# Turning two weight matrices by chunks of rows as they load, in a random-feature attention and MoE kernel

## The chip, the cores and the metric

The kernel runs on one core of one Trainium2 chip. The metric is device time in microseconds from one launch to its end; lower is better. The span in a profile runs from the first to the last instruction of one profiled execution. In this text TensorE is also called PE (and PEld for its weight loads), VectorE DVE, ScalarE ACT, GpSimd POOL and SyncE SP, as the profile does.

## The reference

The input `x` has 4 x 2048 tokens of width 512, normalized to `xn`. The output is `x + attention(xn) + ffn(xn)`. The attention part turns tokens and 512 input-weight rows into 512 random features and multiplies them; the ffn part is a mixture of 64 experts with 8 chosen for each token, plus one shared expert.

```python
def _rfs(xw, ab, AB, gs):
    dot_products = jnp.einsum('...d,rd->...r', xw, ab[:, None] * gs)
    correction = (0.5 * jnp.sum(xw * xw, axis=-1))[..., None] * (ab * ab)
    return 1.0 / math.sqrt(NUM_RFS) * AB * jnp.exp(dot_products - correction)

weights = _rfs(input_weights, xis, jnp.exp(xis), proj_matrix)
feats   = _rfs(xn,            xis, jnp.exp(xis), proj_matrix)
attention = jnp.einsum('bsr,or->bso', feats, weights)

# ffn: sigmoid router, 4 of 8 groups, top 8 of 64 experts, capacity 256 each
g = jnp.einsum('ech,ehi->eci', dispatch, gate_w)
u = jnp.einsum('ech,ehi->eci', dispatch, up_w)
expert_out = jnp.einsum('eci,eih->ech', jax.nn.silu(g) * u, down_w)
sg = jax.nn.silu(tokens @ shared_gate_w) * (tokens @ shared_up_w)
output = scattered_and_weighted(expert_out) + sg @ shared_down_w
```

## The kernel before

Every matrix product is made of three products of `float32r` operands: each operand is split into a high part (`upper`, L98, a cast on ScalarE) and the remainder (`rest`, L101, a subtraction on VectorE), and `products` (L108) adds high by high, high by low and low by high.

Tokens are worked in 16 blocks of 512 rows (`TB`), each of 4 chunks of 128 rows (`NS`); the width of 512 is 4 column chunks (`KC`). Work comes in this order.

*Start.* The input weights `wi` load in four DMAs of 128 rows each, the projection `pj` in two of 256 rows, then token blocks 0 and 1 (`xb`), the router weights `rw_sb` and the shared expert's weights `sgu` and `sd`, all issued from SyncE's queue in this order. GpSimd builds the identity `ident`, a triangle `tri`, ones, and small index tables. `statistics(wi)` (L275, L278) takes means and variances of `wi` on VectorE. `turn` (L331) turns a 512 x 512 matrix: for each column chunk `kc` it makes four transposes, one for each chunk of rows, into one tile of 512 columns in PSUM, and then splits that tile into `hi[kc]` and `lo[kc]`. It is called for `wi`, giving `wT`, and for `pj`, giving `pT`. `projected` multiplies the two into four tiles `ps_f`, one for each chunk `rc` of 128 features. Meanwhile VectorE takes block 0's statistics and inverse roots (`roots`), which are placed behind the last `rest` of `pT`; ScalarE makes the normalized rows `xw` from `shift` (L290, L301); and `turn` is called for them. `as_row` and `across` send a row of squared norms through DRAM (`norms`, L262) and read it back across all partitions as `q` (L267); for the weights this tile is `wn`. `exponent` (L493) on `wn`, an exponential, a scale and one more split (`features_w`) make the attention weights `fW`, in four pieces of their own.

*Dense phase.* For even blocks `dense` computes the shared expert (`ps_gu`, `ps_o`), the features (`ps_f`) and the attention output; `look_up` does the routing, whose logits go through `ps_l`, `lt` (L374) and back through `ps_lt` (L381). Odd blocks are only routed and their turned tiles stored in DRAM (`turned`).

*Experts.* 64 experts are worked one after another: loads of gate and up weights two experts ahead and of down weights one ahead, splits, gathering of tokens, `ps_gu`, `ps_e`, and adding rows into the output. The features of the odd blocks (`ps_fu`, `ps_y`) are computed between them. The last block and the stores end the kernel.

*What sets the order.* The program is written step by step, and a scheduler puts each engine's instructions into one fixed order, with a semaphore wait where data or a buffer is needed; an engine works through its own order and never passes a waiting instruction. `behind(a, b)` adds an order without data between two instructions; `last["upper"]` and `last["rest"]` hold the latest splits for that purpose. Most tiles of 4 KiB a partition (`kib4`) come from one pool, `four`, with `SLOTS4` = 40 slots that are given out again when their tile is read for the last time; a load into a slot waits for that. `wT`, `pT` and `fW` take four slots each: `wT`'s come back after `projected`, those of `pT` and `fW` never. The pool `act` has four buffers with the tag `t`, used by `lt` and other short-lived tiles; `q` has three buffers.

The piece of `turn` that the change replaces for the two weight matrices:

```python
for kc in range(KC):
    pr = pool.tile([P, TB], dt, tag=tag, name="ps_x")
    for s in range(NS):
        last["turn"] = nc.tensor.transpose(pr[:, ts(s, P)], src(s)[:, ts(kc, P)], ident)
    last["upper"] = upper(hi[kc], ps)
    last["rest"] = rest(lo[kc], ps, hi[kc])
```

Of the kernel before, what the change touches and what calls it, by code (L numbers as in the profile page):

```python
# [9 lines left out]
FP = mybir.dt.float32  # L10
FPR = mybir.dt.float32r
I32 = mybir.dt.int32
# [6 lines left out]
P = 128  # L19
# [3 lines left out]
E = 64  # L23
# [8 lines left out]
TB = 512  # L32
NB = T // TB
NS = TB // P
KC = H // P
RC = R // P
IC = I // P
NH = CAP // P
SLOTS4 = 40
UT = TB // 2  # L40
GAP = 5
NCH = T // P
ROUND = 5
TE = 4
TPAD = T + CAP
XW = H + E + 1
# [7 lines left out]
def rfs_attention_moe_kernel(  # L54
# [15 lines left out]
    nc = tc.nc  # L70
    xf = x.flatten_outer_dims()

    const = ctx.enter_context(tc.tile_pool(name="const", bufs=1))
    dram = ctx.enter_context(tc.tile_pool(name="dram", bufs=1, space=DRAM))
    ps_tr = ctx.enter_context(tc.tile_pool(name="ps_tr", bufs=2, space=PSUM))
    ps_mm = ctx.enter_context(tc.tile_pool(name="ps_mm", bufs=4, space=PSUM))
    ps_sm = ctx.enter_context(tc.tile_pool(name="ps_sm", bufs=2, space=PSUM))

    four = ctx.enter_context(tc.tile_pool(name="four", bufs=SLOTS4))
    rows = ctx.enter_context(tc.tile_pool(name="rows", bufs=4))  # L80
    rt = ctx.enter_context(tc.tile_pool(name="rt", bufs=1))
    act = ctx.enter_context(tc.tile_pool(name="act", bufs=4))

    def kib4(shape, name, dt=FPR):
        return four.tile(shape, dt, tag="four", name=name)
# [11 lines left out]
    def upper(dst, src):  # L97
        return nc.scalar.copy(dst, src)  # L98

    def rest(dst, src, hi, on=nc.vector):  # L100
        return on.tensor_tensor(dst, src, hi.bitcast(FP), ALU.subtract)  # L101
# [15 lines left out]
    def behind(a, b):  # L117

        tc.add_manual_dep(a.ins, b.ins.name, ORDER, reason="what a needs comes late")
# [23 lines left out]
    def load_rows(src, name, at_once=2):  # L143

        xb = Chunks(NS, name, FP)
        for k, t in enumerate(xb.t):
            for s in range(0, 2, at_once):
                r0 = (2 * k + s) * P
                nc.sync.dma_start(
                    t[:, s : s + at_once, :],  # L150
                    src[r0 : r0 + at_once * P, :].rearrange("(s p) d -> p s d", p=P),
                )
        return xb

    def load_tokens(b):
        return load_rows(xf[ts(b, TB), :], "xb")
# [8 lines left out]
    last = {}  # L165
    late_blocks = range(1, NB - 1, 2)
    last_stored = late_blocks[-1]
    wi = load_rows(iw, "wi", 1)
    pj = load_rows(proj, "pj")
    xbs = {0: load_tokens(0)}  # L170
    ab = const.tile([P, RC], FP, name="ab")
    nc.sync.dma_start(ab, xis.rearrange("(c p) -> p c", p=P))
    rw_sb = kib4([P, KC, E], "rw_sb", FP)
    nc.sync.dma_start(rw_sb, rw.rearrange("(c p) e -> p c e", p=P))

    def load_shared_gates():
# [15 lines left out]
    ident = const.tile([P, P], FP, name="ident")  # L192
    make_identity(nc, ident)
    ident_r = const.tile([P, P], FPR, name="ident_r")
    nc.gpsimd.tensor_copy(ident_r, ident)
    tri = kib4([P, P], "tri", FP)
    make_upper_triangular(nc, tri, 1.0, diag=True)
    tri_r = const.tile([P, P], FPR, name="tri_r")
    nc.gpsimd.tensor_copy(tri_r, tri)
# [15 lines left out]
    nc.gpsimd.iota(slot_i, pattern=[[P, NH]], base=0, channel_multiplier=1)  # L215
    slot = const.tile([P, NH], FP, name="slot")
    nc.gpsimd.tensor_copy(slot, slot_i)
    erow_i = kib4([P, E], "erow_i", I32)
    nc.gpsimd.iota(erow_i, pattern=[[1, E]], base=-E, channel_multiplier=0)
    erow = const.tile([P, E], FP, name="erow")  # L220
    nc.gpsimd.tensor_copy(erow, erow_i)
# [41 lines left out]

    def across(n):

        q = rt.tile([P, TB], FP, tag="q", name="q", bufs=3)
        nc.sync.dma_start(q, norms[n].partition_broadcast(P))  # L267
        return q

    def statistics(rows_of, after=NS * [None]):  # L270

        mv = rt.tile([P, NS, 2], FP, tag="mv", name="mv", bufs=2)
        for s in range(NS):
            st = rt.tile([P, 6], FP, tag="st", name="st", bufs=4)
            last["stats"] = nc.vector.bn_stats(st, rows_of[s])  # L275
            if after[s] is not None:
                behind(last["stats"], after[s])
            nc.vector.bn_aggr(mv[:, s, :], st)  # L278
        return mv
# [17 lines left out]
    def normalize(b, rstd, shift):  # L297
# [11 lines left out]
        xc = None  # L309
        if b >= ROUND:  # L310

# [10 lines left out]
    def turn(src, name, pools=((ps_tr, "tr"),), after=None, dt=FP):  # L322

        hi = Chunks(KC, name + "_h")
        lo = Chunks(KC, name + "_l")
        for kc in range(KC):
            pool, tag = pools[kc % len(pools)]
            pr = pool.tile([P, TB], dt, tag=tag, name="ps_x")
            ps = pr if dt is FP else pr.bitcast(FP)
            for s in range(NS):  # L330
                last["turn"] = nc.tensor.transpose(  # L331
                    pr[:, ts(s, P)], src(s)[:, ts(kc, P)], ident if dt is FP else ident_r
                )
                if after is not None:
                    behind(last["turn"], after)
                    after = None
            last["upper"] = upper(hi[kc], ps)
            last["rest"] = rest(lo[kc], ps, hi[kc])
        return hi, lo

    xTs = {}

    def look_up(b):

        xw, xc = normed.pop(b)
        xT = turn(
            (lambda s: xc[s // NH][:, s % NH, :].bitcast(FPR))
            if xc
# [166 lines left out]
    def dense(b, xT, whole, w, rows_of):  # L515


        (sgu_h, sgu_l), (sd_h, sd_l) = w
        nsq = across(b) if whole else None
        hT = [kib4([P, IC, TB], "hT") for _ in range(2)]  # L520
        v = parts(xT, KC)
# [55 lines left out]
    def late_attention(blocks):  # L577

        blocks = list(blocks)
        nxt = fetch_block(blocks[0]), across(blocks[0])  # L580
        yield
        for n, b in enumerate(blocks):
            xu, nsq = nxt
            fT = Chunks(RC, "fU"), Chunks(RC, "fU")
            for rc in range(RC):
                ps = ps_sm.tile([P, TB], FP, tag="sm", name="ps_fu")
                feature(fT, parts(xu, KC), nsq, rc, ps)
                yield
            if n + 1 < len(blocks):
                nxt = fetch_block(blocks[n + 1]), across(blocks[n + 1])  # L590
            for s in range(NS):
                if s % 2 == 0:
                    yb = kib4([P, 2, H], "yb", FP)
                po = ps_sm.tile([P, H], FP, tag="sm", name="ps_y")
                attended(po, fT, s, True)
                last["dve"] = nc.vector.tensor_copy(yb[:, s % 2, :], po)
                if "down" in last:
                    behind(last["dve"], last["down"])
                if s % 2:
                    r0 = (b // 2) * TB + (s // 2) * UT  # L600
                    nc.sync.dma_start(
                        attn[r0 : r0 + UT, :].rearrange("(s p) d -> p s d", p=P), yb
                    )
                yield
# [10 lines left out]
        added.append(group)  # L615


    wmv = statistics(wi)
    wT = turn(lambda s: wi[s], "wT", ((ps_tr, "tr"), (ps_sm, "sm")))
    wq = const.tile([P, NS], FP, name="wq")  # L620
    nc.gpsimd.tensor_tensor(wq, wmv[:, :, 0], wmv[:, :, 0], ALU.mult)
    nc.gpsimd.tensor_tensor(wq, wq, wmv[:, :, 1], ALU.add)
    nc.gpsimd.tensor_scalar(padded[2][:, :NS], wq, -0.5 * H, None, ALU.mult)
    as_row(NB, padded[2])
    wn = across(NB)
    pT = turn(lambda s: pj[s], "pT", ((ps_mm, "mm"),))
    rwp = const.tile([P, KC, 2, E], FPR, name="rwp")
    behind(upper(rwp[:, :, 0, :], rw_sb), last["upper"])
    rest(rwp[:, :, 1, :], rw_sb, rwp[:, :, 0, :], nc.gpsimd)
# [6 lines left out]
    def split(t, name, after=(None, None)):  # L636

        hi, lo = kib4(list(t.shape), name + "_h"), kib4(list(t.shape), name + "_l")
        both = upper(hi, t), rest(lo, t, hi)
        last["split"] = both[1]  # L640
        for a, b in zip(both, after):
            if b is not None:
                behind(a, b)
        return hi, lo

    def split_gates(gu):
        return list(zip(*(split(t, "gu") for t in gu)))

    def split_down(d):
        return split(d, "d")  # L650

    sgate = split(sgu[0], "gu", (None, seed1))
    ps_w = []
    for rc in range(RC):
        pool, tag = ((ps_sm, "sm"), (ps_tr, "tr"))[rc // 2]
# [16 lines left out]
    lt0 = last["lt"]  # L672
    shared_w = list(zip(sgate, sup)), split(sd, "d", (lt0, exponents))
    next(late)
    fW = Chunks(RC, "fW_h"), Chunks(RC, "fW_l")

    def features_w(rc):
        f = fw[rc]
# [18 lines left out]
    def find(at, e):  # L697

        for h in range(NH):
            in_turn(  # L700
                nc.gpsimd.indirect_dma_start(  # L701
                    out=at[:, e % TE, h, :],
                    out_offset=None,
# [5 lines left out]
    def tokens_of(n, at, after):  # L709


        sl = slot.unsqueeze(1).to_broadcast([P, TE, NH])
        less = nc.vector.tensor_tensor(
            at, at, sl.unsqueeze(3).to_broadcast([P, TE, NH, P]), ALU.is_le
        )
        behind(less, after)
        tok = rt.tile([P, TE, NH], FP, tag="tok", name="tok", bufs=2)
        nc.vector.tensor_reduce(tok, at, AX.X, ALU.add)
        nc.vector.tensor_tensor(tok, tok, first_of[:, ts(n, TE), :], ALU.add)
        own = rt.tile([P, TE, NH], FP, tag="sown", name="sown", bufs=2)  # L720
        nc.vector.scalar_tensor_tensor(own, tok, float(T), sl, ALU.is_ge, ALU.mult)
# [278 lines left out]
```

## Time and profile before

| what | value |
|---|---|
| median of 3 runs | 1310.99 us (1310.63 to 1311.27) |
| the profiled execution's own time | 1310.94 us |
| its span | 1309.2 us |
| TensorE busy | 1296.7 us, 99% of the span |
| VectorE busy | 925.0 us, 71% |
| ScalarE busy | 645.2 us, 49% |
| GpSimd busy | 581.7 us, 44% |
| granted TensorE clock, mean | 0.999 |

The profiled execution took 1310.94 us, of which 1309.2 are its span and 1.7 lie around it. A row of the timeline gives start and duration of an instruction, or of several equal ones in a row (x4), and in brackets how long the engine stood idle before it and what ended that. A matmul's duration includes its way through the array, and equal ones overlap: their pace is the distance between starts. A row of the waits gives the waiting instruction, what released it, the time in total, how often, and the longest.

### The profile page before, as it was taken

How to read it: one execution, taken by the hardware profiler on the slowest of the kernel's cores; microseconds unless marked ns; L12 is line 12 of the kernel's file. 1: busy time of each engine (PE TensorE's matmuls, PEld its weight loads, DVE VectorE, ACT ScalarE, POOL GpSimd, SP SyncE). 2: the span in 40 equal slices, each digit the busy share in tenths (PEclk: the TensorE clock that was granted, in tenths of full speed). 3: DMA queues.
4: the chain of work that ended last, by engine and by line, in shares of the span. 5: the costliest groups of instructions: out<-in, count | busy, mean ns of one | idle time of the engine just before them, and what ended most of it. 6: DMA issues, size and time to landing. Idle time of an engine off the chain costs nothing.

```text
span 1309.2 us, 21368 instructions
## 1 busy us (share of the span) xinstructions
PE 1296.7 (99%) x7648; PEld 1138.6 (87%) x7648; DVE 925.0 (71%) x1922; ACT 645.2 (49%) x1017; POOL 581.7 (44%) x692
## 2 busy tenths in 40 slices
PE   8999999999999999999999999999999999999998
PEld 6888888888888999999999999999999999988886
DVE  7978768867865776777767677776776676643555
ACT  5643544354432555656566556555665566540111
POOL 3122022123106767877666667767676654210000
PEclk9999999999999999999999999999999999999999
DMA  7665675675586989999999999999999999784995
GB/s 255 242 213 205 244 279 199 238 286 212 201 307 193 317 226 330 259 290 272 304 282 266 292 272 274 246 321 262 282 256 303 280 261 233 206 239 168 318 319 193
DMA packets 189498, 338.61 MB, mean 259 GB/s; under 512 B 15952, under 2 KB 87632, under 8 KB 189392
## 3 DMA queue, kind: packets, MB, share of 16 engines
q1 hardware_dynamic: 153456, 245.93, 54.6%
q0 software_dynamic: 35936, 91.32, 29.7%
q8 instruction: 60, 0.98, 0.3%
q14 instruction: 46, 0.38, 0.1%
HBM read 220.66 MB, written 104.99 MB: 249 GB/s over the span
## 4 chain that ended last, share of the span: by engine, by line
PE 91%; DVE 4%; DMA 2%; SPq 1%; ACT 1%; issue 1%; POOL 0%; DVEq 0%; ACTq 0%
PE ps_gu L108 41%; PE ps_e L108 13%; PE ps_o L108 13%; PE ps_y L108 6%; PE ps_fu L108 6%; PE ps_f L108 4%; PE ps_t L771 3%; PE ps_x L331 2%; PE ps_l L364 2%; DMA xb<-in_L_attn_x_dram 1%; DVE st L275 1%; DMA xT_l<-turned 1%; SPq L262 1%; DVE xT_l L101 1%; DMA gu<-in_L_ffn_up_w_dram 0%
## 5 line engine op out<-in xcount | busy, mean ns | idle before, releaser
L824 POOL DMA_INDIRECT out_dram<-ye,who x128 | 225.3, 1760 | 189.3 <-ACT ye L823 140.9
L108 PE MATMUL ps_gu<-gT,gu_h 128*128 128x256 f32 x2048 | 290.0, 283 | 0.0
L108 PEld LDWEIGHTS ps_gu<-gT,gu_h 128*128 128x128 f32 x2048 | 267.2, 191 | 5.6 <-ACT gu_h L98 1.0
L701 POOL DMA_INDIRECT at<-upto,line x128 | 138.0, 1078 | 76.0 <-DVE first_of L695 37.3
L108 PE MATMUL ps_gu<-gT,gu_l 128*128 128x256 f32 x1024 | 167.0, 285 | 0.0
L101 DVE TENSOR_TENSOR gu_l<-gu,gu_h 128x1024 fp32r<-128x1024 f32 x128 | 155.7, 1218 | 6.9 <-ACT gu_h L98 6.9
L754 POOL DMA_INDIRECT xg<-xnw,who x128 | 137.3, 1073 | 39.0 <-issue 32.0
L108 PE MATMUL ps_e<-d_h,ehT 128*128 128x512 f32 x512 | 148.5, 391 | 0.0
L108 PEld LDWEIGHTS ps_gu<-gT,gu_l 128*128 128x128 f32 x1024 | 140.7, 191 | 0.3
L98 ACT CAST gu_h<-gu 128x1024 fp32r<-128x1024 f32 x128 | 132.4, 1058 | 0.0
L98 ACT CAST ehT<-sg 128x512 fp32r<-128x512 f32 x64 | 39.7, 621 | 156.3 <-DVE sg L501 156.3
L823 ACT ACTIVATE ye<-ps_e,we 128x512 f32<-128x512 f32 x128 | 88.6, 694 | 57.0 <-PE ps_e L108 56.1
L108 PEld LDWEIGHTS ps_e<-d_h,ehT 128*128 128x128 f32 x512 | 94.7, 188 | 18.8
L246 POOL TENSOR_TENSOR a<-rstd,ve 128x4 f32<-128x4 f32 x45 | 10.5, 233 | 200.1 <-DVE rstd L242 197.6
L501 DVE SCALAR_TENSOR_TENSOR sg<-sg,ps_gu 128x512 f32<-128x512 f32 x64 | 43.9, 686 | 68.4 <-PE ps_gu L108 68.0
L507 ACT ACTIVATE f<-f,ab 128x512 f32<-128x512 f32 x64 | 46.3, 723 | 82.0 <-DVE f L493 81.3
L101 DVE TENSOR_TENSOR d_l<-d,d_h 128x1024 fp32r<-128x1024 f32 x64 | 78.2, 1222 | 7.8 <-ACT d_h L98 7.4
L101 DVE TENSOR_TENSOR gT<-ps_t,gT 128x512 fp32r<-128x512 f32 x128 | 83.2, 682 | 0.2 <-ACT gT L98 0.2
L101 DVE TENSOR_TENSOR ehT<-sg,ehT 128x512 fp32r<-128x512 f32 x64 | 44.3, 692 | 51.5 <-ACT ehT L98 51.5
L108 PE MATMUL ps_o<-fW_h,fT 128*128 128x512 f32 x288 | 80.0, 392 | 0.2 <-ACT fT L98 0.2
L108 PE MATMUL ps_e<-d_l,ehT 128*128 128x512 f32 x256 | 79.3, 391 | 0.0
L108 PE MATMUL ps_o<-d_h,hT 128*128 128x512 f32 x256 | 79.1, 396 | 0.0
(181 smaller groups left out, 2526.8 us busy)
## 6 DMA issues: line engine op xcount, KB each, us to landing
gu<-in_L_ffn_gate_w_dram SPq DMA_DIRECT2D x64, 512.0 KB
gu<-in_L_ffn_up_w_dram SPq DMA_DIRECT2D x64, 512.0 KB
d<-in_L_ffn_down_w_dram SPq DMA_DIRECT2D x64, 512.0 KB
xnw<-xw SPq DMA_DIRECT2D x32, 577.0 KB
xb<-in_L_attn_x_dram SPq DMA_DIRECT2D x32, 512.0 KB
out_dram<-xb SPq DMA_DIRECT2D x32, 512.0 KB
xT_h<-turned SPq DMA_DIRECT2D x30, 512.0 KB
xT_l<-turned SPq DMA_DIRECT2D x30, 512.0 KB
```

What stands on the lines that cost most here:

```text
L98: return nc.scalar.copy(dst, src)
L101: return on.tensor_tensor(dst, src, hi.bitcast(FP), ALU.subtract)
L108: last["pe"] = nc.tensor.matmul(ps, w[c][a], v[c][b], start=(start and part == 0 and c == 0), stop=(stop and part == 2 and c == n - 1),)
L331: last["turn"] = nc.tensor.transpose(pr[:, ts(s, P)], src(s)[:, ts(kc, P)], ident if dt is FP else ident_r)
L364: logits = nc.tensor.matmul(pl, rwp[:, kc].rearrange("p t e -> p (t e)"), v[kc], start=(n == 0 and kc == 0), stop=(n == 1 and kc == KC - 1),)
L501: nc.vector.scalar_tensor_tensor(dst, dst, 0.5, u, ALU.mult, ALU.mult)
L507: nc.scalar.activation(f, f, AF.Exp, scale=ab[:, rc : rc + 1])
L701: nc.gpsimd.indirect_dma_start(out=at[:, e % TE, h, :], out_offset=None, in_=upto, in_offset=bass.IndirectOffsetOnAxis(ap=line[:, e, h : h ...
L754: nc.gpsimd.indirect_dma_start(out=xgs[e][:, h, :], out_offset=None, in_=xnw, in_offset=bass.IndirectOffsetOnAxis(ap=who[:, e, h : h + 1], ...
L771: turned_s = nc.tensor.transpose(pr[:, c, ts(h, P)], xr[:, h, ts(c2 * 2 + c, P)], ident_r)
L823: nc.scalar.activation(ye[:, h, :], po, AF.Copy, scale=wes[e][:, h : h + 1])
L824: now = nc.gpsimd.indirect_dma_start(out=out, out_offset=bass.IndirectOffsetOnAxis(ap=who[:, e, h : h + 1], axis=0), in_=ye[:, h, :], in_o ...
```

## The change

`wi` and `pj` are now turned chunk of rows by chunk of rows. A new function, `turn_as_loaded`, makes the four transposes of one chunk of 128 rows, one for each column chunk, into one PSUM tile, and splits it into the 128 columns `ts(s, P)` of `hi` and `lo`. Its outputs are tiles of 4 x 512 in the pool of constants, written 128 columns at a time in each of the four column chunks. `pj` loads in four DMAs of 128 rows. Ahead of the first chunk stand ten transposes of the identity into a PSUM tile that nobody reads. `statistics(wi)` is now written behind both turns. `fW` takes the place of `wT` once `wT` has been used. To make room, `four` has 33 slots instead of 40, `rw_sb`, `tri` and `erow_i` are taken from `act`, and `q` has two buffers. `split` now also records its `upper` in `last`, so that what is placed behind the latest `upper` may come behind that one.

```diff
-SLOTS4 = 40
+SLOTS4 = 33
+WARM = 10
...
-    pj = load_rows(proj, "pj")
+    pj = load_rows(proj, "pj", 1)
...
-    rw_sb = kib4([P, KC, E], "rw_sb", FP)
+    rw_sb = act.tile([P, KC, E], FP, tag="t", name="rw_sb")
...
-    tri = kib4([P, P], "tri", FP)
+    tri = act.tile([P, P], FP, tag="t", name="tri")
...
-    erow_i = kib4([P, E], "erow_i", I32)
+    erow_i = act.tile([P, E], I32, tag="t", name="erow_i")
...
-        q = rt.tile([P, TB], FP, tag="q", name="q", bufs=3)
+        q = rt.tile([P, TB], FP, tag="q", name="q", bufs=2)
...
+    def turn_as_loaded(src, hi, lo, pools):
+        for s in range(NS):
+            pool, tag = pools[s % len(pools)]
+            ps = pool.tile([P, KC, P], FP, tag=tag, name="ps_x")
+            for kc in range(KC):
+                last["turn"] = nc.tensor.transpose(ps[:, kc, :], src[s][:, ts(kc, P)], ident)
+            to = hi[:, :, ts(s, P)], lo[:, :, ts(s, P)]
+            last["upper"] = upper(to[0], ps)
+            last["rest"] = rest(to[1], ps, to[0])
...
+    warm = ps_mm.tile([P, TB], FP, tag="mm", name="ps_0")
+    for n in range(WARM):
+        nc.tensor.transpose(warm[:, ts(n % NS, P)], ident, ident)
+    wT = [const.tile([P, KC, TB], FPR, name=f"wT_{n}") for n in "hl"]
+    turn_as_loaded(wi, *wT, ((ps_tr, "tr"), (ps_sm, "sm")))
+    wT = [[t[:, c, :] for c in range(KC)] for t in wT]
+    pT = [const.tile([P, KC, TB], FPR, name=f"pT_{n}") for n in "hl"]
+    turn_as_loaded(pj, *pT, ((ps_mm, "mm"),))
+    pT = [[t[:, c, :] for c in range(KC)] for t in pT]
     wmv = statistics(wi)
-    wT = turn(lambda s: wi[s], "wT", ((ps_tr, "tr"), (ps_sm, "sm")))
...
     wn = across(NB)
-    pT = turn(lambda s: pj[s], "pT", ((ps_mm, "mm"),))
...
-        last["split"] = both[1]
+        last["upper"], last["split"] = both
...
-    fW = Chunks(RC, "fW_h"), Chunks(RC, "fW_l")
+    fW = wT
```

## The prediction

> **What bounds the kernel now.** I read the page's busy shares, then who TensorE waits for over the whole span, then the start engine by engine, since the diff edits mostly the start.
>
> ```profile
> PE 1296.7 (99%) x7648; PEld 1138.6 (87%) x7648; DVE 925.0 (71%) x1922; ACT 645.2 (49%) x1017; POOL 581.7 (44%) x692
> ```
>
> TensorE is busy 1296.7 of 1309.2 us, so only 12.5 us are idle. Its waits, longest in total first (engine, line waited for: us in total, times, longest):
>
> ```profile
> PE ps_x L331 <- DMA wi<-_attn_input_weights_dram: 5.1, 3, 3.7
> PE ps_bu L445 <- DVE prior_r L435: 0.9, 3, 0.3
> PE ps_lt L381 <- ACT lt L374: 0.6, 2, 0.4
> ```
>
> The only large named wait is at the very start. TensorE's own timeline there (start us, us, line, out<-in, count):
>
> ```profile
> 3.67 1.02 PE L331 MATMUL ps_x<-ident,wi 128*128 128x128 f32 x2 [3.67 <-DMA wi<-_attn_input_weights_dram]
> 5.89 0.47 PE L331 MATMUL ps_x<-ident,wi 128*128 128x128 f32 x1 [1.20 <-DMA wi<-_attn_input_weights_dram]
> 6.56 3.04 PE L331 MATMUL ps_x<-ident,wi 128*128 128x128 f32 x13 [0.20 <-DMA wi<-_attn_input_weights_dram]
> 9.39 3.29 PE L331 MATMUL ps_x<-ident,pj 128*128 128x128 f32 x16
> 12.44 1.42 PE L108 MATMUL ps_f<-wT_h,pT_h 128*128 128x512 f32 x5
> ...
> 23.48 1.91 PE L331 MATMUL ps_x<-ident,xw 128*128 128x128 f32 x16
> ...
> 32.90 0.66 PE L381 MATMUL ps_lt<-ident,lt 128*128 128x128 f32 x4 [0.40 <-ACT lt L374]
> ```
>
> The first column of chunks needs all four row chunks, so one transpose is done per arrival and 13 are left at 6.56. They start every (9.39-6.56)/13 = 0.218 us; those of `xw` later (25.1-23.48)/15 = 0.11. The pace halves the cost, and the tile's answer (ns min/median/max) shows when it changed:
>
> ```profile
> L331 PE MATMUL ps_x<-ident,pj x16: 272/421/421, 9.4 to 12.4; 128*128 128x128 f32 x16
> L331 PE MATMUL ps_x<-ident,xw x16: 270/272/273, 23.5 to 25.1; 128*128 128x128 f32 x16
> ```
>
> The last `pj` transpose already ran at 272 ns. From 12.44 on, 48 matmuls `ps_f` start 0.226 us apart and end at 23.48 with no gap. VectorE at the same time:
>
> ```profile
> 6.70 0.66 DVE L275 BATCH_NORM_STATS2 st<-wi 128x6 f32<-128x512 f32 x1
> 7.39 0.18 DVE L278 BATCH_NORM_AGGREGATE mv<-st 128x2 f32<-128x6 f32 x1
> 7.69 0.69 DVE L101 TENSOR_TENSOR wT_l<-ps_x,wT_h 128x512 fp32r<-128x512 f32 x1
> 8.54 0.69 DVE L101 TENSOR_TENSOR wT_l<-ps_x,wT_h 128x512 fp32r<-128x512 f32 x1 [0.16 <-ACT wT_h L98]
> ...
> 14.02 1.28 DVE L275 BATCH_NORM_STATS2 st<-xb 128x6 f32<-128x512 f32 x2
> ...
> 20.06 0.17 DVE L290 TENSOR_SCALAR shift<-shift 128x4 f32<-128x4 f32 x1
> ...
> 24.73 2.48 DVE L101 TENSOR_TENSOR xT_l<-ps_x,xT_h 128x512 fp32r<-128x512 f32 x4
> ```
>
> The eight `wT_l`/`pT_l` come every 0.857 us, at the pace of four slow transposes, although back to back they take (27.14-24.73)/4 = 0.60, as `xT_l` shows. Block 0's statistics wait in order behind them. The chain that ended last has the same story:
>
> ```profile
> 12.19 0.60 ACT pT_h L98
> 12.81 1.29 DVE pT_l L101 x2
> 14.10 1.19 DVE st L275 x2
> ...
> 32.37 0.48 ACT lt L374
> 32.90 0.66 PE ps_lt L381 x4
> ```
>
> It leaves TensorE at 12.19, goes through VectorE's statistics and roots, GpSimd's roots of block 1, ScalarE's `xw` and `lt`, and comes back to TensorE at 32.90. From there on TensorE carries it nearly alone.
>
> **The change, part by part.** The instruction order of both builds is known: VectorE still has the four statistics of `wi` first, then the eight `rest`s, then the moved `sq` transpose, then block 0's statistics.
>
> Warm-up. The identity is ready at 1.44 (its select starts at 1.14 and takes 0.30). Ten transposes at 0.218 end near 3.65; the first rows of `wi` are used at 3.56. Cover: TensorE's idle 3.67 us. Without it, at most 2.2 us. I take 0.
>
> What they warm. The Trainium skill, TensorE: Matmul & The Clock Gate, Part 4 (PE-mode transpose), says that transposes do not count as activity for the clock gate, so that it would not open for them: a rule against this change. The row above says otherwise: only transposes had run when the last `pj` one fell to 272 ns, 5.7 us after the unbroken run began at 6.56. (The granted clock reads 1.00 throughout, so this shows in durations alone.) I follow the row. By row: fast pace well before 9 us. By rule: 0.218 throughout, priced below.
>
> Chunk order on TensorE. Chunks of `wi` arrive at about 3.6, 4.2, 5.9, 6.6 and four transposes go with each; the last four end by 7.0 (fast) or 7.6 (slow). `pj` must arrive next. The last chunk of `wi` landed at 6.56 when, by the stretches, about 1.42 MB had moved for 1.05 MB of `wi`: a lag of 1 us at 0.38 MB/us. The 2.1 MB of `wi` and `pj` have moved at 5+(2.1-0.85)/0.38 = 8.3, so `pj` ends at about 9.3 (estimate). With four fast transposes `ps_f` starts at 9.8 in place of 12.44 and ends at 9.8+10.9 = 20.7 instead of 23.48. TensorE alone would gain 2.7 us. By the rule, 16 slow ones from 7.6 end at 11.1, and `ps_f` at 22.0.
>
> VectorE. The statistics of `wi` follow the loads and still end at 7.57. `wT_h` of chunk 0 is there by then, so eight `rest`s run back to back: 7.6+8x0.60 = 12.4, plus 0.1 for `sq`: block 0's statistics start at 12.5, not 14.02. Even at slow transposes `pT_h` 3 ends at 11.1+0.2+0.6 = 11.9, just when VectorE reaches its `rest`. So the gain is 1.5 us by row or rule, and this is the shorter of the two chains.
>
> Where the stall goes. `shift` comes at 18.6, `xw` is complete at 23.2-1.5 = 21.7. TensorE, done at 20.7, waits about 1 us there (three of its transposes can go in it). By the rule it comes at 22.0, 0.3 late, so the rule's sum would be at most 0.3 us worse. Next, roots of block 1 on GpSimd, `xw` and `lt` keep the same 1.5 us, so `ps_lt` starts at 31.4. TensorE's extra lead of up to a microsecond is lost there, the 0.40 wait growing to about 0.8.
>
> Loads. Four `pj` issues in place of two add 2x0.45 = 0.9 us on SyncE's queue, ahead of both `xb` loads, `ab` and `rw_sb`. The engines of the DMA are already full (share 1.04 from 5 us), so the data behind queues anyway; `xb` 0 (3.15 MB with all before it; 2.76 had moved at 10, then about 0.3 per us) has moved by 11.3, and its second half is read at 13.7. Bounds 0 and 0.9; I take 0. The moved `sq` is 1.5 us later (10.86 to 12.4); its four `norms` writes start at 15.88 on SyncE, behind the `zrow` stores and a load, so they and the `q` read at 23.68 keep their times. `q` is now read from 26.8 instead of 28.28; transfers stop by 27.0, so 0 to 0.3 late, covered by VectorE's 1.4 us wait for `eab`.
>
> Buffers, 0 each with bounds. `four` loses seven slots while eight held for the whole run (`pT`, `fW`) leave it: 32 rotating become 33, one load further ahead; worth at most TensorE's 1.2 us of waits for `gu_h`. `q` with two buffers: `wn` is read out by 31 and the next `q` but one comes much later; block 15's `q` moves from before the experts to near their end, long before use. `rw_sb`, `tri`, `erow_i` in `act` are read out by 14, the next tile there is `lt` at 32. `fW` in `wT`'s place waits for `ps_f` (20.7) and is written from about 35. New order of `eab` and `fw` splits on ScalarE and VectorE: the same instructions, -0.3 to 0.5. Strided outputs 128x4x128: the strided read of `ps_lt` (L389, 256 elements) took 0.42, as does L404 with as many, so 0.
>
> Sum: -1.5, all else 0. Profiled: 1310.94 with span 1309.2; its span becomes 1307.7. The median is 1310.99, practically the same run, so 1309.5.
>
> **The rivals.** (a) TensorE's own gain counts: 2.7 us, 1308.3. For: it is the bound of 99% of the span. Against: 48 `ps_f` cannot bring `xw` forward, and VectorE's order is fixed. (b) The gain is lost at the next fixed arrival: `sgu` lands at 17.35 and ScalarE casts it until 18.4 ahead of `xw`, 0.2 us before `shift`; if it lands 0.9 late with the longer issue, `xw` loses 0.7, and with `q` late another 0.3: gain 0.5, 1310.5. For: both margins are thin. Against: full DMA engines. (c) Slower: the strided writes of the 16 splits run slower. It decides when a pair's pace on VectorE passes (14.0-0.1-7.6)/8 = 0.79 us; at twice 0.60 block 0's statistics start at 7.6+9.6+0.1 = 17.3, 3.3 late: 1314.3. For: no row has this very write. Against: the strided row above.
>
> **How the numbers follow.** Forecast 0.66, (a) 0.12, (b) 0.14, (c) 0.08. 0.2% is 2.6 us, about what a measurement of this kernel can tell from no change: faster means under 1308.4, slower over 1313.6. The forecast lies inside with either bound of its small terms, (b) too; (a) is at the edge and mostly beyond with the slot's bound; so faster 0.12, same 0.80, slower 0.08. The range takes the forecast, (b) and the nearer part of (a): 1308.3 to 1311.3; its upper end has 0.9 for the late loads and 0.5 for the new order on (b)'s 1310.5, less what they share.
>
> **What would show it.** Right: ten transposes from 1.5; 272 ns ones before 9; `ps_f` from 9.8; VectorE's eight `rest`s at 0.60, block 0's statistics at 12.5; a TensorE wait of about 1 us for `xw`; `ps_lt` at 31.4 and all later work 1.5 us early. Wrong: the `rest`s slower than 0.70; statistics waiting for `xb`; `ps_lt` at 30.5 or earlier, or after 32.5; a new TensorE wait later than 40 us.

## The result: slower by 0.4%, lost one product at a time

The changed kernel takes 1316.18 us (median of 6 runs, 1315.86 to 1316.73), the kernel before 1311.29 in the same comparison (6 runs): a ratio of 1.0038, 95% interval 1.0028 to 1.0048. The prediction was 1309.5, with a range up to 1311.3. The start became shorter by 1.1 us, where 1.5 was predicted; the rest, which was to stay as it was, became longer by 7 us. Three executions in the comparisons below took over 2000 us and are left out of every number.

### The profile page after: what moved, and what is told of

Same layout as the page of the kernel before. It is cut to its first block, busy times and chain, and to the rows that moved or that the text cites. A ratio compares the mean times of both kernels' runs of the same rounds, so it can differ in the third digit from the quotient of the medians.

```text
span 1314.9 us, 21338 instructions
## 1 busy us (share of the span) xinstructions
PE 1305.5 (99%) x7658; PEld 1138.7 (87%) x7658; DVE 925.9 (70%) x1922; ACT 645.6 (49%) x1017; POOL 588.0 (45%) x692
## 4 chain that ended last, share of the span: by engine, by line
PE 96%; DMA 2%; DVE 1%; SPq 1%; issue 0%; ACT 0%; DVEq 0%
PE ps_gu L109 41%; PE ps_o L109 14%; PE ps_e L109 13%; PE ps_f L109 7%; PE ps_y L109 6%; PE ps_fu L109 6%; PE ps_t L792 3%; PE ps_l L377 2%; PE ps_x L332 2%; DMA sd<-L_ffn_shared_down_w_dram 1%; PE ps_lt L394 1%; PE ps_bu L469 0%; DMA wi<-_attn_input_weights_dram 0%; DMA xb<-in_L_attn_x_dram 0%; DMA q<-norms 0%; DMA norms<-sq 0%
## 5 line engine op out<-in xcount | busy, mean ns | idle before, releaser
L845 POOL DMA_INDIRECT out_dram<-ye,who x128 | 228.2, 1783 | 188.1 <-ACT ye L844 126.8
L109 PE MATMUL ps_o<-wT_h,fT 128*128 128x512 f32 x288 | 81.6, 396 | 0.0
```

What stands on the lines that cost most here:

```text
L109: last["pe"] = nc.tensor.matmul(ps, w[c][a], v[c][b], start=(start and part == 0 and c == 0), stop=(stop and part == 2 and c == n - 1),)
L845: now = nc.gpsimd.indirect_dma_start(out=out, out_offset=bass.IndirectOffsetOnAxis(ap=who[:, e, h : h + 1], axis=0), in_=ye[:, h, :], in_o ...
```

## The profile after

The busy shares of the changed kernel:

```profile
PE 1305.5 (99%) x7658; PEld 1138.7 (87%) x7658; DVE 925.9 (70%) x1922; ACT 645.6 (49%) x1017; POOL 588.0 (45%) x692
```

TensorE has ten more matmuls (the warm-up transposes, 2.4 us) and is busy 8.8 us longer; its span is 1314.9 us in place of 1309.2. VectorE and ScalarE work as long as before. TensorE's waits over the whole span:

```profile
PE ps L634 <- POOL ident masks.py:199: 1.5, 1, 1.5
PE ps_gu L109 <- DVE xT_l L102: 0.9, 1, 0.9
PE ps_l L377 <- DVE fw L506: 0.5, 1, 0.5
PE ps_x L349 <- DMA wi<-_attn_input_weights_dram: 0.4, 1, 0.4
```

No wait explains a loss of 6 us: the 5.1 us for `wi` have become 1.5 for the identity and 0.4 for `wi`, and what is new is 0.9 and 0.5. So the time is not idle time. TensorE's timeline at the start:

```profile
1.50 2.39 PE L634 MATMUL ps<-ident 128*128 128x128 f32 x10 [1.50 <-POOL ident masks.py:199]
3.69 1.91 PE L349 MATMUL ps_x<-ident,wi 128*128 128x128 f32 x8
5.96 1.68 PE L349 MATMUL ps_x<-ident,wi 128*128 128x128 f32 x8 [0.36 <-DMA wi<-_attn_input_weights_dram]
7.91 2.67 PE L349 MATMUL ps_x<-ident,pj 128*128 128x128 f32 x16 [0.27 <-DMA pj<-_L_attn_proj_matrix_dram]
10.33 1.17 PE L109 MATMUL ps_f<-wT_h,pT_h 128*128 128x512 f32 x4
...
21.32 1.91 PE L332 MATMUL ps_x<-ident,xw 128*128 128x128 f32 x16
24.09 1.24 PE L109 MATMUL ps_gu<-xT_h,gu_h 128*128 128x512 f32 x4 [0.86 <-DVE xT_l L102]
...
28.90 1.17 PE L377 MATMUL ps_l<-xT_h,rwp 128*128 128x512 f32 x4 [0.48 <-DVE fw L506]
...
31.76 0.60 PE L394 MATMUL ps_lt<-ident,lt 128*128 128x128 f32 x4
```

`ps_f` starts at 10.33 in place of 12.44, `ps_lt` at 31.76 in place of 32.90: a lead of 1.14 us. The pace of the transposes by tile (min/median/max):

```profile
L349 PE MATMUL ps_x<-ident,wi x16: 272/417/472, 3.7 to 7.4; 128*128 128x128 f32 x16
L349 PE MATMUL ps_x<-ident,pj x16: 272/273/332, 7.9 to 10.3; 128*128 128x128 f32 x16
```

Those of `pj` run at 272 ns almost from the first, with nothing but transposes ahead of them. VectorE, whose chain the forecast was built on:

```profile
7.78 2.45 DVE L102 TENSOR_TENSOR wT_l<-ps_x,wT_h 128x512 fp32r<-128x512 f32 x4
10.15 2.47 DVE L102 TENSOR_TENSOR pT_l<-ps_x,pT_h 128x512 fp32r<-128x512 f32 x4
12.54 0.20 DVE L260 STREAM_TRANSPOSE sq<-padded 128x32 f32<-128x32 f32 x1
12.66 1.24 DVE L276 BATCH_NORM_STATS2 st<-xb 128x6 f32<-128x512 f32 x2
...
18.67 0.17 DVE L291 TENSOR_SCALAR shift<-shift 128x4 f32<-128x4 f32 x1
...
28.01 2.73 DVE L506 SCALAR_TENSOR_TENSOR fw<-q,ab,ps_f 128x512 f32<-128x512 f32 x4 [0.94 <-DMA q<-norms]
```

Eight `rest`s in 4.76 us (0.60 each), strided outputs included; block 0's statistics at 12.66, `shift` at 18.67. `fw` waits 0.94 us for `q`; in the kernel before, VectorE's wait ahead of `fw` was another:

```profile
DVE coef L670 <- ACT eab L668: 1.4, 1, 1.4
```

The chain that ended last, between 10 and 34 us, no longer goes through VectorE's roots:

```profile
12.35 8.11 DMA sd<-L_ffn_shared_down_w_dram
20.45 0.02 issue
20.47 3.57 DMA norms<-sq
24.04 0.02 issue
24.06 3.85 DMA q<-norms
...
28.01 0.76 DVE fw L506
28.77 0.14 issue
28.90 2.08 PE ps_l L377 x8
```

A store of the norms waits for the load of `sd`, the read of `q` for the norms, `fw` for `q`, and `ps_l` stands behind it: this is where part of the predicted gain stayed, 1.1 us in place of 1.5.

The rest shows when the same matmul is looked up in both traces (start after minus start before):

| start in the kernel before, us | 33 | 94 | 150 | 240 | 380 | 600 | 900 | 1200 |
|---|---|---|---|---|---|---|---|---|
| changed kernel's lag, us | -1.1 | -0.7 | -0.1 | +0.8 | +1.2 | +3.0 | +4.0 | +5.9 |

Nothing jumps; the lead leaks away. A stretch of block 2's features shows how. Kernel before:

```profile
97.00 1.07 PE L108 MATMUL ps_f<-xT_h,pT_l 128*128 128x512 f32 x4
...
103.35 1.91 PE L331 MATMUL ps_x<-ident,xw 128*128 128x128 f32 x16
```

Changed kernel:

```profile
96.35 1.10 PE L109 MATMUL ps_f<-xT_h,pT_l 128*128 128x512 f32 x4
...
102.88 1.91 PE L332 MATMUL ps_x<-ident,xw 128*128 128x128 f32 x16
```

Between the two rows lie the same 28 matmuls: 6.35 us, 226.8 ns each, before; 6.53 us, 233.2 ns each, after. Neither has a gap. Summed from start to start by operand, from the first `ps_lt` on: the 768 products with `pT` cost 3.76 us more, the 768 with `fW` (which now lies in `wT`'s place) 2.89, those with `rwp` 0.12 less, all others 0.41 more. That is 6.9 us, less the lead of 1.1: the 5.7 us by which the span grew, to 0.1. What the change did to those two operands is to give them another place in SBUF, the on-chip memory. Each product reads two operands there: the weights, which PEld loads, and the moving operand, which the matmul itself reads.

## Experiments

**First set: which part does it?** Four readings were stated: A, the operands' distance modulo 128 bytes; B, the place itself; C, fewer slots and buffers; D, the new order at the start.

The small pads below are tiles that nobody reads; one behind `who`, the last constant ahead of the pool, shifts `four`. The comments behind `#` are mine.

```diff
+    gap_e = const.tile([P, 8], FP, name="gap_e")     # 32 bytes, behind who
+    nc.gpsimd.memset(gap_e, 0.0)
```

> The changed kernel with one 32-byte constant tile more behind `who`, so that the pool `four` starts 32 bytes later and every operand of its tiles lies at the same offset within 128 bytes (64) as `wT` and `pT` do. Nothing else moves. Theory A (relative offset: a 512-column product runs at 227 ns when its moving operand and its weights start at the same offset within 128 bytes, and at about 233 when they are 32 bytes apart): the 1536 products with `pT` or `fW` return from 233 to 227 ns, 7 us are gained, about 1309.5 to 1310.2, that is 1.1 us under before. Theory B (place: the low addresses of the constants are slow in themselves) and theory C (fewer slots and two `q` buffers cost time all along): the products stay at 233 ns and the time at 1316.2.

Measured: 1315.5 us (1315.18 to 1317.11), ratio 1.0033 (1.0021 to 1.0046). A as stated, modulo 128, is wrong.

```diff
-SLOTS4 = 33
+SLOTS4 = 32
+    gap_p = const.tile([P, 8], FP, name="gap_p")     # between wT and pT; gap_e as above
+    nc.gpsimd.memset(gap_p, 0.0)
```

> The changed kernel with 32 bytes between `wT` and `pT` and 32 bytes behind `who`: `pT` lies at the same offset as the tiles of `four` (96), `wT`, and so `fW`, 32 bytes below (64). `four` has 32 slots, since the space ends there. Theory A: products with `pT` at 227 ns, those with `fW` at 233 to 234; of the 7.2 us that the two groups lost, 3.8 (pT) come back and 2.9 (fW) stay: about 1312.5. Theories B and C: both groups at 233, 1316.2 or later.

Measured: 1316.6 us (1316.03 to 1316.89), ratio 1.0038 (1.0024 to 1.0052). Wrong again.

The kernel before, with nothing changed but its buffers (excerpt):

```diff
-SLOTS4 = 40
+SLOTS4 = 33
+    fixed = {m: [const.tile([P, KC, TB], FPR, name=f"{m}_{n}") for n in "hl"] for m in ("wT", "pT")}
...
-    fW = Chunks(RC, "fW_h"), Chunks(RC, "fW_l")
+    fW = wT
...
-        q = rt.tile([P, TB], FP, tag="q", name="q", bufs=3)
+        q = rt.tile([P, TB], FP, tag="q", name="q", bufs=2)
```

> The kernel before with the placement alone: `wT` and `pT` in two constant tiles each at the addresses of the changed kernel, `fW` in `wT`'s place, 33 slots, two `q` buffers, `rw_sb`, `tri`, `erow_i` in `act`; turning, loads and their order as before, no warm-up. Theories A and B: products with `pT` and `fW` at 233 ns, 7 us lost and nothing gained at the start: about 1318.3. Theory D (the new order at the start costs time later): 1311.3.

Measured: 1322.13 us (1321.38 to 1322.62), ratio 1.008 (1.0064 to 1.0097). D is out: without the new order the loss is all there, and 3.8 us more than expected. Its trace puts that surplus at the start, where TensorE lags by 4.0 us at 33 us. The largest part is one wait:

```profile
PE ps_gu L108 <- ACT gu_h L98: 2.8, 1, 2.8
```

ScalarE's order had changed with the buffers: it casts this `gu_h` at 29.13 us, behind the first `xw` of block 1, and in the kernel before at 26.02, ahead of it. Behind the wait the granted clock, 1.00 up to 31 us, reads 0.67, 0.50, 0.50 and 0.63 in the four microseconds from 31 to 35 us and 1.00 again from 35 on; the time lost to it is some 1.7 us (an estimate from these four figures). From 33 us to the end the run loses 7.2 us more, where the changed kernel loses 6.9.

```diff
-SLOTS4 = 33
+SLOTS4 = 32
+    gap_e = const.tile([P, 24], FP, name="gap_e")    # 96 bytes, behind who
+    nc.gpsimd.memset(gap_e, 0.0)
```

> The changed kernel with 96 bytes behind `who` and 32 slots: `wT` and `pT` at offset 64 within 128 bytes, the tiles of `four` at 0, so 64 apart. If only the offset within 64 bytes counts, 227 ns and about 1310. If any difference within 128 bytes counts alike, 233 ns and 1316.2. If it is as for `rwp` in the kernel before (64 apart from its moving operand, mean 230.6 ns), about 230 to 231 and 1313.5. Theories B and C: 1316.2 or later.

Measured: 1314.07 us (1313.69 to 1314.84), ratio 1.002 (1.0012 to 1.0027), between two of the variants. Its rows gave the clue (columns: count, busy us, mean ns of one). The kernel before:

```profile
L108 PE MATMUL ps_f<-xT_l,pT_h 128*128 128x512 f32 x144 | 38.6, 390 | 0.0
L108 PE MATMUL ps_o<-fW_l,fT 128*128 128x512 f32 x144 | 39.4, 392 | 0.0
```

This run:

```profile
L109 PE MATMUL ps_f<-xT_l,pT_h 128*128 128x512 f32 x144 | 39.4, 395 | 0.0
L109 PE MATMUL ps_o<-wT_l,fT 128*128 128x512 f32 x144 | 39.8, 393 | 0.0
```

The changed kernel:

```profile
L109 PE MATMUL ps_f<-xT_l,pT_h 128*128 128x512 f32 x144 | 39.5, 396 | 0.0
L109 PE MATMUL ps_o<-wT_l,fT 128*128 128x512 f32 x144 | 40.5, 399 | 0.0
```

With all three at multiples of 64 bytes, `wT` is mostly cured and `pT` not at all. In `ps_f<-xT,pT` the weights are `pT` and the moving operand comes from `four`; in `ps_o<-wT,fT` it is the other way round. So the sign of the distance matters, and 64 one way is not 64 the other way: the period is longer than 128. I took each product of 512 columns, and sorted its gap to the next start by one number: the address of the weights that are loaded for the next product, minus the address of the moving operand, modulo 256 bytes. The addresses are those that each program gives its tiles when it is built; the traces have none. The table has the kernel before, the changed one, these four runs, and the four of the last set; gaps from 40 us on between two such products, without those over 250 ns, which I take for waits.

| distance modulo 256 | gaps | mean ns | share over 229 ns |
|---|---|---|---|
| 0 | 24579 | 228.0 | 21% |
| 192 | 966 | 230.2 | 53% |
| 128 | 2089 | 232.6 | 73% |
| 64 | 698 | 233.3 | 98% |
| 160 | 2271 | 233.6 | 99% |
| 96 | 2172 | 233.7 | 96% |

Classes modulo 128 account for 27% of the variance of these gaps, modulo 256 for 37%, modulo 512 for no more. It fits all four runs: "equal" in the first meant 128 apart; in the second `pT` was 128 and `wT` 160 off; in the fourth `pT` 64 and `wT` 192; the third lay as the changed kernel does. In the kernel before, `wT`, `pT`, `fW` and their partners all came from slots of 4 KiB of one pool, 0 apart; the change made it 160 for `pT` and 96 for `fW`.

**Second set: equal modulo 256.** A sort after the fact is no test, so the next kernels were built from it. The three tiles `wq`, `eab` and `coef` take 96 bytes between `pT` and `four`; allocated ahead of `wT`, they bring `wT`, `pT` and `rwp` to 160 modulo 256, where `four` is.

```diff
+    wq = const.tile([P, NS], FP, name="wq")
+    eab = const.tile([P, RC], FP, name="eab")
+    coef = const.tile([P, RC], FP, name="coef")
     wT = [const.tile([P, KC, TB], FPR, name=f"wT_{n}") for n in "hl"]
...
-    wq = const.tile([P, NS], FP, name="wq")
...
-    eab = const.tile([P, RC], FP, name="eab")
...
-    coef = const.tile([P, RC], FP, name="coef")
```

> The changed kernel with three small tiles (wq, eab, coef: 96 bytes in all) allocated ahead of wT instead of behind pT. Nothing grows and no instruction is added or reordered; wT, pT and rwp now start at the same byte offset modulo 256 as the slots of `four` (160). Theory E, read out of the traces of the first four runs: a product of 512 columns runs at 227 to 228 ns where the address of the weights loaded for the next product minus the address of the moving operand is a multiple of 256 (mean 228.3 ns over 12166 gaps), at 232.6 ns where it is 128 off, at 233.5 ns where it is 32, 64, 96 or 160 off, whatever the place; so the first run's 64 and 192 were no equals. E expects all the losses of the products with wT and pT (2.9 and 3.8 us) and 0.3 us of rwp back: 1309.3 to 1310.5 us. Theory B (the low addresses, or the tiles of 8 KiB, are slow in themselves) expects 1315.5 to 1316.5, as wT and pT stay where they are to within 96 bytes.

In this set TensorE's mean granted clock was 0.991 to 0.997, in the kernel before too (in this run's trace it fell to 0.89 from 400 to 440 us), so its times of some 1327 to 1330 us compare only to about 0.2%. Measured: ratio 1.0003 (0.9984 to 1.0021). The paces tell more: the products with `pT` and `wT` were back at those of the kernel before (mean gap of `ps_f<-xT_l,pT_h` 227.4 ns, of `ps_o<-wT_l,fT` 226.8).

With the three tiles between `wT` and `pT` instead, only `pT` is equal:

> The same, but the three small tiles lie between wT and pT: pT and rwp start equal modulo 256 to the slots of `four`, wT stays 96 bytes off. Theory E expects that products with pT are back at 227 to 228 ns (3.8 us) and those with wT stay at 233 to 235 ns: 1311.8 to 1312.8 us, between the changed kernel and the run with all equal, nearer to the latter by 3.8 to 2.9. Theory B expects 1315.5 to 1316.5. In the prologue ps_f<-wT,pT, which ran at 227 ns with both at the same offset, is expected at about 233 ns by E: 48 x 6 ns = 0.3 us.

Measured: ratio 1.0032 (1.0012 to 1.0052): at B's value, with an interval that reaches E's as well. In the trace the products with `pT` were cured and those with `wT` were not.

Without the warm-up, on the kernel with all equal:

```diff
-    warm = ps_mm.tile([P, TB], FP, tag="mm", name="ps_0")
-    for n in range(WARM):
-        nc.tensor.transpose(warm[:, ts(n % NS, P)], ident, ident)
```

> The run with all equal modulo 256, without the ten transposes of the identity. Theory F: they do not lie on the path, since the eight rests on VectorE of 0.6 us each from 7.8 us on set when ps_f starts: 0 to +0.2 us against the run with them. Theory G: they bring TensorE's pace up before the rows of wi arrive; without them the transposes of wi go at some 420 instead of 270 ns while cold, the last of them up to 1 us later, and ps_f with it: +0.5 to +1.3 us.

Measured: ratio 1.0006 (0.9988 to 1.0023), too wide to decide between F and G. In the trace, `pj`'s transposes had a median of 339 ns (273 with the warm-up), and `ps_f` started at 10.36 in place of 10.19 us: up to there it is F. But `ps_lt` came at 31.99 in place of 31.11 us. `fw` had waited 1.30 us for `q`, with the warm-up 0.42, so this is a later `q` and not slower transposes; whether leaving out the warm-up makes `q` late is not shown. What the warm-up is worth stays open.

The zero rows' stores behind the read of `q`, also on the kernel with all equal:

```diff
-    for n in range(NH):
-        nc.sync.dma_start(xnw[T + n * P : T + n * P + P, :], zrow)
-    for n in range(NH):
-        nc.sync.dma_start(out[T + n * P : T + n * P + P, :], zrow[:, :H])
...
     wn = across(NB)
+    for n in range(NH):
+        nc.sync.dma_start(xnw[T + n * P : T + n * P + P, :], zrow)
+    for n in range(NH):
+        nc.sync.dma_start(out[T + n * P : T + n * P + P, :], zrow[:, :H])
```

> The run with all equal modulo 256, with the four stores of the zero rows issued behind the norms of the weights (across(NB)) instead of ahead of them. In the changed kernel VectorE waited 0.94 us for q<-norms and TensorE then 0.48 us for fw at 28.9 us. Theory H: q is late because each of the small stores of the norms takes the place of the eighth transfer before it, the loads of sgu and sd; with the zero rows behind them they take the places of xb, ab and rw: q lands 1 us or more earlier, the wait of 0.48 us goes, and the run is 0.3 to 0.6 us shorter than the one with all equal: about 1309.4. Rival: the split of the second operand (the wait of 0.86 us for xT_l at 24.1 us) or the logits' chain set the same point anyway, or the freed places change nothing: 0 us.

Measured: ratio 0.9992 (0.9972 to 1.0012), too wide to tell it from the run with all equal.

**Third set: the same on a chip with a steady clock.** The kernel before took 1311.05 us there.

> The kernel with the three small tiles ahead of wT (all operands equal modulo 256), once more, for its time: in the run before this the granted clock fell to 0.99 for part of every execution, of the kernel before too, and its comparison is only good to 0.2%. In its trace the products with wT and pT were back at 227 to 228 ns and TensorE led the kernel before by 1.8 us at 33 us and 2.9 us at 380 us, ahead of the dip in the clock. Theory E expects 1308.6 to 1309.8 us where the kernel before takes 1311.3 (ratio 0.9980 to 0.9990); theory B 1315.5 or more (1.003).

Measured: 1309.42 us (1308.56 to 1310.75, 21 runs), ratio 0.9989 (0.9982 to 0.9995), as E expected. The changed kernel with three small tiles moved is 0.1% faster than the kernel before, where as it stands it is 0.4% slower. The stretch of block 2's features in its timeline:

```profile
95.74 1.07 PE L109 MATMUL ps_f<-xT_h,pT_l 128*128 128x512 f32 x4
...
102.09 1.91 PE L332 MATMUL ps_x<-ident,xw 128*128 128x128 f32 x16
```

28 matmuls in 6.35 us again, 226.8 ns each. TensorE's lead is 1.3 us at 33 us, 1.7 at 380 and 1.9 at 1300: what the start gains is kept. The half microsecond on top of it is pace: 0.35 with `rwp`, which lay 192 off in the kernel before, and 0.21 with `pT`. B is refuted: the tiles lie where they were to within 96 bytes. So is C: slots and buffers are those of the changed kernel.

> pT alone equal modulo 256, wT 96 bytes off, once more for its time. Theory E: 2.9 us (products with fW) and 48 x 6 ns in the prologue more than the run with all equal: 1311.8 to 1313.0 us, ratio 1.0004 to 1.0014; theory B 1315.5 or more.

Measured: 1313.03 us (1312.33 to 1314.29), ratio 1.0016 (1.0009 to 1.0023), at the upper end of E's range (time and ratio a little above it), and 3.6 us over the run with all equal, where 3.2 were expected. Its rows, `pT` and then `wT`:

```profile
L109 PE MATMUL ps_f<-xT_l,pT_h 128*128 128x512 f32 x144 | 38.6, 390 | 0.0
L109 PE MATMUL ps_o<-wT_l,fT 128*128 128x512 f32 x144 | 40.6, 399 | 0.0
L109 PE MATMUL ps_f<-wT_l,pT_h 128*128 128x512 f32 x16 | 4.4, 396 | 0.0
```

The first is as in the kernel before (390), the second as in the changed one (399), and the third, the prologue's product of the two, now slow, though it was not in the changed kernel (389): there both lay equally. One operand at a time, each product follows its own pair.

> All equal modulo 256 and the zero rows' stores behind the norms of the weights, once more for its time. In its trace q was issued at 21.0 instead of 23.7 us and VectorE no longer waited for it, but TensorE's lead at 33 us was 1.85 us against 1.78: 0 to 0.2 us less than the run with all equal. The rival, that the earlier q is worth the whole wait of 0.4 us: 0.4 to 0.6 us less.

Measured: 1309.16 us (21 runs, lowest 1307.69), ratio 0.9986 (0.9979 to 0.9992). `q` in its trace:

```profile
L502 DVE SCALAR_TENSOR_TENSOR fw<-q,ab,ps_f x4: 742/743/743, 26.7 to 28.7; 128x512 f32<-128x512 f32 x4
L264 SPq DMA_DIRECT2D q<-norms x2: 320/332/344, 20.9 to 32.0; - x2
```

The read is issued at 20.9 us (24.1 in the changed kernel) and `fw` starts at 26.7 (28.0) without a wait for it. TensorE's lead at 33 us is 1.7 us against 1.3, of which 0.2 came from an earlier `ps_f` (10.03 against 10.26), and the time is 0.26 us less, within the noise. In the second set's traces the leads were 1.85 and 1.78. So the late `q` is worth 0.1 to 0.2 us by these two pairs of traces, and no time shows it; between two traces of the kernel with all equal the lead itself differed by 0.5 (1.78 and 1.3).

> The kernel before with the changed kernel's buffers, as in the run of the placement alone, but with the three small tiles ahead of wT, so that wT, pT and rwp are equal modulo 256 to `four`. In the placement run TensorE lost 4.0 us by 33 us (2.8 us of it waiting for gu_h, from the old order in fewer slots) and 7 us more over the rest. Theory E expects that only the second loss goes: 1322.1 - 7.0 = 1315.1, 1314.6 to 1315.6 us, with the wait for gu_h still there. If the fewer slots or the buffers of 8 KiB cost time in themselves over the span, 1317 or more.

Measured: 1314.34 us (1311.89 to 1315.71, 9 runs), ratio 1.0023 (1.0014 to 1.0033): 7.8 us less than with the same buffers 96 bytes off, 0.3 below the range. The wait for `gu_h` is still there:

```profile
29.88 0.50 PE L108 MATMUL ps_gu<-xT_h,gu_h 128*128 128x512 f32 x1 [2.71 <-ACT gu_h L98]
```

Behind 33 us TensorE lost nothing: it lags by 2.1 us there and by 1.0 at the end. So the trace shows no cost of the fewer slots or of the tiles of 8 KiB over the span. The traced execution is the fastest of the nine, and in it the granted clock stayed at 1.00 behind the wait. Its mean was 0.999 in the three executions below 1313 us and 0.998 in the six from 1314 us on, which fits the dip of the clock that the run of the placement alone has in its trace (0.998 in all four of its executions); none of the six has a trace.

## Why the prediction was wrong

- *Warm-up, and the row against the rule.* Right: ten transposes from 1.50, at 417 ns, then 272 ns from 7.9 us, before the 9 us named, with only transposes run. Without the ten, the same 16 transposes of `pj` had a median of 339 ns in place of 273. So the rule set against the row did not hold here.
- *Chunk order on TensorE.* Right in kind, 0.5 late: `pj` came later than the estimate, `ps_f` at 10.33 in place of 9.8. It cost nothing there: VectorE came to `xT_l` at 23.34 straight from other work. In the trace of the run with all equal VectorE was earlier and waited 0.42 us for `xT_h`, so there the time of `ps_f` counted.
- *VectorE.* Right to 0.2 us: eight `rest`s at 0.60, statistics at 12.66 for 12.5, `shift` at 18.67 for 18.6. Rival (c), slow strided writes, is refuted by the same rows. *Loads, 0*, was right for `xb`: the statistics did not wait for it.
- *The stall.* The wait of about 1 us came, but at `xT_l` (0.86), one step behind `xw`.
- *`q`, "0 to 0.3 late, covered".* Under-sized: VectorE waited 0.94 and TensorE 0.48. The prediction moved `sq` later and kept `q`'s time, but let `fw`, its reader, come 1.5 us earlier without a matching cover: the wait for `eab` had been that cover, and it is no longer among VectorE's waits. The read itself was issued at 24.06 and not at 23.68 us. The lead was 1.4 us at `shift` and 1.1 at `ps_lt`; by the experiments the late `q` is 0.1 to 0.2 of what went between (part of rival (b)).
- *"Buffers, 0 each".* This is the step that failed, by 6.65 us. It asked when each buffer is free, and never where it is. `pT` and `fW` were moved out of the pool of their partners, to 160 and 96 bytes modulo 256 from them, and their 1536 products went from 228 ns to between 233 and 234 wherever nothing else was waited for; over all of them, waits included, that came to 6.65 us. With 99% of the span on TensorE, each of these is on the path. With the same buffers, `wT` and `pT` 96 bytes further on, the loss is gone (1309.42 us).
- *The rivals.* None had it. The result lies where the prediction put 0.08, over 1313.6 us, but what that chance stood for, (c), did not happen. "A new TensorE wait later than 40 us" was named as a sign of error; none is among the waits, because the loss is in the pace.
- *The number without that step.* With all operands equal the kernel took 1309.42 us, where 1309.5 had been forecast. That is in part luck: the start gave 1.3 us for 1.5, and the half microsecond of pace was in no sum.

What stays open is why. The Trainium skill (TensorE: Matmul & The Clock Gate, Part 2: What happens when you issue a matmul) says that the moving operand and the weight load have two independent read ports of SBUF, so that loading the next weights takes nothing from a running matmul. The runs here show a pace that depends on the distance of the two; the measurement decides. Whether it is the next product's weights or the present one's could not be separated (both account for 37% of the variance), what the other 63% are was not looked into, and no run changed the data type or the number of columns. Nor is it settled what the remaining 0.4 us of the other products was.

## What to carry to other kernels

When a change takes an operand into another pool, compare addresses as well as sizes: on this kernel, bound by TensorE, three small tiles in front decided whether two operands' products ran at 228 or 233 ns. If a loss shows in no wait, line up the same instruction in both traces and look whether the lag jumps or creeps; a creep points to pace, and start-to-start gaps by operand find whose. And a cover named for a late transfer must be checked again once its reader moves earlier.

## What was not expected of the hardware

- Products of 128x512 in `float32r` ran at 228.0 ns on average where weights and moving operand lie equally modulo 256 bytes, and at 232.6 to 233.7 ns at 64, 96, 128 and 160 off; 192 off was in between (230.2). The absolute offset mattered by 1 ns at most: pairs with a distance of 0 ran at 228.8, 227.8, 228.3 and 228.7 ns with both at 0, 160, 192 and 224.
- Three small tiles, 96 bytes, allocated ahead instead of behind changed the whole time by 0.5% (changed kernel, 1.0038 to 0.9989) and 0.6% (placement alone, 1.008 to 1.0023).
- Behind a wait of 2.8 us the granted clock was 0.50 to 0.67 for some 4 us in one trace; behind one of 2.71 us it stayed at 1.00 in another.
